# Reordering the start of a GRU and mixture-of-experts kernel: first loads, biases and the second block's projections

## The chip, the cores and the metric

The kernel runs on one core of one Trainium2 chip. The metric is device time in microseconds (us) of one execution; the median of three runs is 1541.6 us (1538.61 to 1542.06).

## What is computed

The input is x with 8 sequences of 256 steps and 512 features. A GRU runs over the steps of every sequence, its outputs go through a mixture of 8 experts (two chosen per token) plus a shared feed-forward part, and x is added to that. What matters here is the GRU cell:

```python
def cell(h, x):
    gi = x @ W_ih + b_ih
    gh = h @ W_hh + b_hh
    i_r, i_z, i_n = jnp.split(gi, 3, axis=-1)
    h_r, h_z, h_n = jnp.split(gh, 3, axis=-1)
    r = jax.nn.sigmoid(i_r + h_r)
    z = jax.nn.sigmoid(i_z + h_z)
    n = jnp.tanh(i_n + r * h_n)
    h_new = (1.0 - z) * n + z * h
```

`gi` doesn't depend on h, so it can be made ahead of the steps. The two biases of r and z can be added together into `gi`; of n, only b_ih goes into `gi`, and the last third of b_hh has to stay with `h_n`.

## The kernel before, in words

The 256 steps are cut into 16 blocks of 16 steps. For a block, x is a tile of 128 tokens by 512 features (`load_x`, L106). `transpose_x` (L256) turns it with four TensorE transposes into PSUM, ScalarE copies that to `xT` (L261), and the load of the block two further on is issued. `project(k, g)` (L294) makes the third g of the block's `gi`: four pieces, one for each 128 features of x, each of four matmuls of 32 columns of weights by 512 (`multiply`, L267; a float32 matmul shows as two records in the trace), and after the last piece VectorE adds the bias (L310) and, for the second and third g, SP issues a DMA of `gi` to DRAM (`gid_rz`, L319, `gid_n`, L321). `load_seeds` (L332) fetches it back in the layout of the steps, four steps at a time, `open_gate` (L349) has ScalarE copy one step's part into the three PSUM banks of the gates, and `step` (L360) multiplies the state by w_hh on top of it (three times 16 matmuls, L368), after which VectorE and ScalarE work out the new state.

The order of all of this is written by hand: every engine takes its instructions in the order in which the program issues them, and waits in place for what the next one needs. Ahead of the loop the program issues, in order, the loads and constants (L111 to L230), the transposes and projections of block 0 (L788 to L791), the transposition of the first state (L792), the seeds of the first eight steps (L794), the opening of the gates of step 0 (L798, in the order r, n, z) and the loads of the shared weights (L799). Then come the blocks. Everything that TensorE does beside the steps is cut into pieces that wait in `queue`; after each step, pieces are taken from it so that the block's share is spread evenly over its 16 steps (L851). Block 0 takes the projections of the next blocks, up to a quota of 2.8 times the cost of one (L831); later blocks take an even part of what is left, and the shared feed-forward part of the block before. Costs are counted in us: `MM` is 0.86 for a piece, `TR` 0.12 for a transpose.

The loads at the start: SP issues the three thirds of w_ih (L118, 1024 KB each), the four parts of w_hh (L132, 768 KB each) and the x of block 1 (L133). ScalarE issues the x of block 0 (L111). GpSimd (POOL) issues b_ih, broadcast from DRAM to all 128 partitions (L123), the first two thirds of b_hh in the same way (L125), the four parts of the first state h (L130), and later the last third of b_hh (L216). VectorE adds the two broadcast biases (L211).

Of the kernel before, what the change touches and what calls it, by code (L numbers as in the profile page):

```python
# [9 lines left out]
F32 = mybir.dt.float32  # L10
# [3 lines left out]
ALU = mybir.AluOpType  # L14
# [3 lines left out]
P = 128  # L18
# [7 lines left out]
def kernel(  # L26
# [46 lines left out]
    nc = tc.nc  # L73
    B, T, D = x.shape
# [4 lines left out]
    NQ = D // P  # L79
    NB = T // TS  # L80
# [17 lines left out]
    ps_mm = ctx.enter_context(tc.tile_pool(name="ps_mm", bufs=3, space=PSUM))  # L98
# [7 lines left out]
    def load_x(k, queue=nc.sync):  # L106
        xt = xpool.tile([P, D], F32, tag="x", name=f"x_{k}")
        queue.dma_start(xt, x[:, k * TS : (k + 1) * TS, :])
        x_tiles[k] = xt

    load_x(0, nc.scalar)  # L111


    we = wts.tile([P, E, NW, D], F32, name="we")
    wih = we[:, E - 2 : E].rearrange("p e w n -> p (e w n)").rearrange("p (q n) -> p q n", q=NQ)
    whh = we[:, E - 4 : E - 2].rearrange("p e w n -> p (e w n)").rearrange("p (q n) -> p q n", q=NQ)
    for g in range(3):
        nc.sync.dma_start(  # L118
            wih[:, :, g * D : (g + 1) * D],
            w_ih[:, g * D : (g + 1) * D].rearrange("(q p) n -> p q n", p=P),  # L120
        )
    bias = const.tile([P, G3], F32, name="bias")
    nc.gpsimd.dma_start(bias, b_ih.partition_broadcast(P))  # L123
    bias_h = we[:, 0, 0:2].rearrange("p w n -> p (w n)")
    nc.gpsimd.dma_start(bias_h, b_hh[0 : 2 * D].partition_broadcast(P))  # L125
    h = state.tile([P, NQ, 32], F32, name="h")
    nc.vector.memset(h, 0.0)
    h0v = h0.rearrange("b (q j i) -> b j q i", q=NQ, j=4)
    for j in range(4):
        nc.gpsimd.dma_start(h[32 * j : 32 * j + B], h0v[:, j])  # L130
    for q in range(NQ):
        nc.sync.dma_start(whh[:, q, :], w_hh[q * P : (q + 1) * P, :])  # L132
    load_x(1)  # L133
    wg = wts.tile([P, NQ, E], F32, name="wg")
    wsu = [wts.tile([P, NQ, 2, IM], F32, name=f"wsu_{c}") for c in range(NSH)]
    wsd = [wts.tile([P, NF, D], F32, name=f"wsd_{c}") for c in range(NSH)]
# [39 lines left out]
    def counting(name, n, base, step, channel):  # L176
# [31 lines left out]
        ]  # L208
        for i in range(NB)
    ]  # L210
    nc.vector.tensor_tensor(  # L211
        bias[:, 0 : 2 * D], bias[:, 0 : 2 * D], bias_h, ALU.add
    )
    b_hn = b_hh[2 * D : G3].rearrange("(q j i) -> j q i", q=NQ, j=4)
    for j in range(4):
        nc.gpsimd.dma_start(  # L216
# [39 lines left out]
    def transpose_x(k):  # L256
        ps = for_transposes([NQ, P], f"xTp_{k}")
        for q in range(NQ):
            nc.tensor.transpose(ps[:, q, :], x_tiles[k][:, q * P : (q + 1) * P], ident)  # L259
        xT = two.tile([P, NQ, P], F32, tag="xrT", name=f"xT_{k}")  # L260
        nc.scalar.copy(xT, ps)  # L261
        xT_of[k] = xT
        x_tiles.pop(k)
        if k + 2 < NB:
            load_x(k + 2)

    def multiply(ps, lhs, rhs, start, stop):  # L267


        for c in range(4) if by_groups[0] else (slice(0, P),):  # L270
            rows_ = slice(32 * c, 32 * c + 32) if by_groups[0] else c
            nc.tensor.matmul(  # L272
                ps[rows_], lhs[:, rows_], rhs, start=start, stop=stop, skip_group_check=True
            )
# [4 lines left out]
    def matmul_piece(issue, end=None):  # L279

        def part(cols, last):
            issue(cols)
            if last and end is not None:
                end()

        return (
            MM,
            lambda: part(slice(0, D), True),  # L290
            [(MM / 2, lambda i=i: part(HALVES[i], i == 1)) for i in range(2)],
        )

    def project(k, g):  # L294

        box = {}

        def issue(q, cols):
            if q == 0 and cols.start == 0:
                box["ps"] = ps_mm.tile([P, D], F32, tag="mm", name=f"gip_{k}_{g}")  # L300
            multiply(
                box["ps"][:, cols],
                xT_of[k][:, q, :],
                wih[:, q, g * D + cols.start : g * D + cols.stop],
                start=(q == 0 and cols.start == 0),
                stop=(q == NQ - 1 and cols.stop == D),
            )

        def end():
            nc.vector.tensor_tensor(  # L310
                gi[:, :, g, :].rearrange("p j (q i) -> p j q i", i=32),
                box["ps"].rearrange("p (q j i) -> p j q i", j=4, i=32),
                bias[:, g * D : (g + 1) * D].rearrange("p (q j i) -> p j q i", j=4, i=32),
                ALU.add,
            )
            if g > 0:
                to = gi_dram[k][g % 2].rearrange("j b t n -> (b t) j n")
                if g == 1:
                    nc.sync.dma_start(to.rearrange("p j (a n) -> p j a n", a=2), gi[:, :, 0:2, :])  # L319
                else:  # L320
                    nc.sync.dma_start(to, gi[:, :, 2, :])  # L321
                    projected.add(k)

        return [
            matmul_piece(lambda cols, q=q: issue(q, cols), end if q == NQ - 1 else None)
            for q in range(NQ)
        ]
# [131 lines left out]
    def weigh_all(k):  # L459

        ch, w2 = chosen.pop(k), weight_of.pop(k)
        comb = said_0[:, :, 1]
        nc.vector.tensor_scalar(comb, ch[:, 0, :], w2[:, 0:1], None, ALU.mult)
        nc.vector.scalar_tensor_tensor(comb, ch[:, 1, :], w2[:, 1:2], comb, ALU.mult, ALU.add)
        nc.vector.tensor_scalar(
            said_0[:, :, 0], row_of.broadcast_to([P, E]), 0.0, None, ALU.add
        )
# [29 lines left out]
    def enter(k, i):  # L497

        pl = places_of[k]
        nc.gpsimd.indirect_dma_start(  # L500
            out=listed.rearrange("r p v -> (r p) v"),
            out_offset=bass.IndirectOffsetOnAxis(ap=pl[:, i : i + 1], axis=0),
            in_=(said[k % 2] if k else said_0)[:, i, :],
            in_offset=None,
        )
# [281 lines left out]

    transpose_x(0)  # L788
    for g in range(3):
        for piece in project(0, g):  # L790
            piece[1]()  # L791
    nc.vector.transpose(states[0].rearrange("p q b -> p (q b)"), h.rearrange("p q i -> p (q i)"))  # L792
    for c in range(NS):
        load_seeds(c)  # L794
# [6 lines left out]
    projections = deque()  # L801
    projections.append((NQ * TR, lambda: transpose_x(1)))
    for k in range(1, NB):
        for g in range(3):
            projections.extend(project(k, g))
            if g == 1 and k + 1 < NB:
                projections.append((NQ * TR, lambda k=k: transpose_x(k + 1)))
    PROJECT = 12 * MM + NQ * TR
    for k in range(NB):


        at = {}

        def when(t, cost, work):
            at.setdefault(t, []).append((cost, work))

        if k > 0:
            steps_ = ((choose, 0.95), (order_experts, 0), (weigh, 0), (give_places, 0.1), (send_rows, 0.5))
            for t, (f, cost) in enumerate(steps_):
                when(t, cost, lambda f=f, k=k: f(k - 1))  # L820
            if k == 1:
                when(3, 0, lambda k=k: weigh_all(k - 1))
            for i in range(2 if k > 1 else E):
                when(i + 4, 0, lambda k=k, i=i: enter(k - 1, i))
            when(6, 0, lambda k=k: load_again(k - 1))
        if 1 <= k <= E - 4:
            when(6, 0, lambda k=k: load_expert(k - 1))
        if k == NB - 1:
            for e in (E - 2, E - 1):
                when(6, 0, lambda e=e: load_expert(e))  # L830
        quota = 2.8 * PROJECT if k == 0 else sum(p[0] for p in projections) / max(1, NB - 1 - k)  # L831
        while projections and quota > 0:
            quota -= projections[0][0]
            queue.append(projections.popleft())
        assert k == NB - 1 or len(projections) <= 13 * (NB - 2 - k), "the next block's are made"
        if k > 0:
            for c in range(NSH):
                feed_at_once(shared_unit(k - 1, c, NSH))
        over = 0.0
        for t in range(TS):  # L840
            n = k * TS + t
            step(n)
            if (n + 1) % SC == 0 and n + 1 < T:
                turn_seeds((n + 1) // SC)
                if (n + 1) // SC + NS - 1 < T // SC:
                    load_seeds((n + 1) // SC + NS - 1)
            for _, work in at.get(t, ()):
                work()

            later_on = sum(cost for s, pieces in at.items() if s >= t for cost, _ in pieces)  # L850
            room = (sum(p[0] for p in queue) + later_on) / (TS - t) - over  # L851
            room -= sum(cost for cost, _ in at.get(t, ()))
            while queue and room > 0.25 * MM:
                if len(queue[0]) > 2 and room < 0.75 * MM:
                    queue.extendleft(reversed(queue.popleft()[2]))
                piece = queue.popleft()
                piece[1]()
                room -= piece[0]
            over = -room if t < TS - 1 else 0.0
        fill()  # L860
# [3 lines left out]
    k = NB - 1  # L864
# [14 lines left out]
    while queue or routing:  # L879
        while routing and (spent >= routing[0][0] or not queue):  # L880
            routing.pop(0)[1](k)
        piece = queue.popleft()
# [36 lines left out]
```

## Time and profile before

| | us |
|---|---|
| median of three runs | 1541.6 (1538.61 to 1542.06) |
| the profiled execution | 1535.54 |
| its span | 1533.8 |
| TensorE busy | 1472.5 (96% of the span) |
| VectorE, ScalarE, GpSimd busy | 731.0, 435.5, 210.2 |
| start of the first projection's matmuls | 14.22 |
| start of step 0's matmuls | 35.61 |

The profile is one execution. The chain that ended last is followed back from the last instruction to whatever released each one, and "issue" in it is time in which an engine waited for nothing that the profile shows. "SPq", "ACTq" and "POOL ... DMA" are instructions that issue DMAs. A row of the timeline has start, length, engine, line, operation, output<-inputs and a count, and in brackets the idle time before it with what ended it. A row of a table of stretches has the length of the stretch, then the busy time and number of instructions of PE, PEld, DVE, ACT and POOL, then the granted TensorE clock as a share of full speed, the share of the DMA engines that was busy, and GB/s. A row of waits has who waited for whom, us in total, how many times, and the longest.

### The profile page before, as it was taken

Reading aid. Unit: us, or ns where it says so; the run is one execution under the profiler, and the core shown is the slowest. Engines: PE = TensorE matmul, PEld = TensorE weight load, DVE = VectorE, ACT = ScalarE, POOL = GpSimd, SP = SyncE. Lnnn points to the kernel's source line nnn. Section 1 sums busy time; section 2 is a strip of 40 time slices with the busy share of each in tenths; the row PEclk is TensorE's granted clock in tenths of the full one; section 3 lists DMA queues with packets and bytes.
Section 4 is the critical chain, followed back from the end, with each engine's and each line's share of the span. In section 5 each row is a group of like instructions: output and inputs, shape, how many; then the busy total and the mean of one; then the engine's idle time right before and its main releaser. Section 6 shows DMA issues by size and latency. Waiting matters only on the chain.

```text
span 1533.8 us, 82162 instructions
## 1 busy us (share of the span) xinstructions
PE 1472.5 (96%) x36779; PEld 1155.0 (75%) x36779; DVE 731.0 (48%) x2747; ACT 435.5 (28%) x1799; POOL 210.2 (14%) x419
## 2 busy tenths in 40 slices
PE   4999799999999999999999999999999999999997
PEld 1677678887879897879787989798889886444443
DVE  2455354545555545555555555555555553222222
ACT  1233232323232323333333333333333331222221
POOL 2001100000000000000000000100010102444443
PEclk9999999999999999999999999999999999999998
DMA  7613112121211111111111110101010214454544
GB/s 255 207 41 110 13 40 64 46 72 42 75 40 36 35 42 34 42 29 41 26 50 28 43 37 26 48 22 49 21 48 22 76 59 141 83 89 90 93 86 62
DMA packets 59168, 94.51 MB, mean 62 GB/s; under 512 B 8960, under 2 KB 29504, under 8 KB 58816
## 3 DMA queue, kind: packets, MB, share of 16 engines
q1 hardware_dynamic: 48056, 66.89, 15.1%
q0 software_dynamic: 10624, 22.10, 7.9%
q8 instruction: 290, 4.75, 1.3%
q14 instruction: 62, 0.51, 0.1%
q10 hardware_dynamic: 136, 0.26, 0.1%
HBM read 57.85 MB, written 31.37 MB: 58 GB/s over the span
## 4 chain that ended last, share of the span: by engine, by line
PE 95%; issue 2%; DMA 1%; ACT 0%; SPq 0%; DVE 0%; POOLq 0%; POOL 0%; DVEq 0%; ACTq 0%
PE ps_r L368 15%; PE gu_s L659 15%; PE ps_n L368 15%; PE ps_z L368 15%; PE gip L272 11%; PE gu_t L595 9%; PE po L272 7%; PE yp L731 4%; PE lgp L419 1%; DMA x<-in_x_dram 1%; PE xTp L259 1%; PE hrp L512 1%; PE ps_r L712 0%; PE ps_z L712 0%; PE ps_n L712 0%
## 5 line engine op out<-in xcount | busy, mean ns | idle before, releaser
L368 PE MATMUL ps_r<-we,hT 128*8 128x128 f32 x8192 | 294.8, 273 | 17.6 <-ACT ps_r L355 9.5
L368 PE MATMUL ps_z<-we,hT 128*8 128x128 f32 x8192 | 299.2, 273 | 5.6 <-issue 4.9
L368 PE MATMUL ps_n<-we,hT 128*8 128x128 f32 x8192 | 297.1, 273 | 2.9 <-issue 2.3
L368 PEld LDWEIGHTS ps_r<-we,hT 128*8 128x8 f32 x8192 | 240.4, 90 | 76.9 <-issue 32.8
L659 PE MATMUL gu_s<-hc,wsu 128*32 128x128 f32 x8192 | 281.0, 274 | 8.3 <-issue 7.9
L659 PEld LDWEIGHTS gu_s<-hc,wsu 128*32 128x32 f32 x8192 | 253.0, 110 | 30.1 <-issue 20.9
L368 PEld LDWEIGHTS ps_z<-we,hT 128*8 128x8 f32 x8192 | 242.2, 90 | 13.2 <-issue 11.5
L368 PEld LDWEIGHTS ps_n<-we,hT 128*8 128x8 f32 x8192 | 241.7, 90 | 8.7 <-issue 7.5
L387 ACT ACTIVATE r<-rT 128x32 f32<-128x32 f32 x256 | 58.6, 229 | 571.5 <-DVE rT L379 565.9
L407 POOL COPY hc<-hT 128x32 f32<-128x32 f32 x256 | 62.0, 242 | 1113.1 <-DVE hT L404 1113.1
L379 DVE STREAM_TRANSPOSE rT<-ps_r 128x128 f32<-128x128 f32 x256 | 80.8, 316 | 272.0 <-PE ps_r L368 271.1
L272 PE MATMUL gip<-we,xT 128*32 128x512 f32 (+1 forms) x1904 | 190.3, 516 | 1.4 <-ACT xT L261 1.4
L379 DVE STREAM_TRANSPOSE nT<-ps_n 128x128 f32<-128x128 f32 x256 | 81.1, 317 | 144.4 <-PE ps_n L368 144.2
L595 PE MATMUL gu_t<-we,xrT 128*128 x312 | 146.7, 593 | 0.2 <-ACT xrT L714 0.2
L272 PE MATMUL po<-wsd,act_s 128*32 128x512 f32 (+2 forms) x1108 | 138.8, 537 | 1.4 <-issue 1.4
L272 PEld LDWEIGHTS gip<-we,xT 128*32 128x32 f32 x1904 | 59.8, 110 | 66.3 <-issue 54.4
L355 ACT COPY ps_n<-seed_hn 128x128 f32<-128x128 f32 x256 | 69.0, 269 | 104.1 <-DVE nT L379 103.0
L379 DVE STREAM_TRANSPOSE zT<-ps_z 128x128 f32<-128x128 f32 x256 | 81.0, 316 | 18.1 <-PE ps_z L368 9.8
L588 DVE TENSOR_TENSOR act_t<-gu_t,act_t 128x256 f32<-128x256 f32 x39 | 16.5, 424 | 146.3 <-ACT act_t L587 146.3
L595 PEld LDWEIGHTS gu_t<-we,xrT 128*128 128x128 f32 x312 | 53.3, 190 | 38.7 <-issue 38.0
L395 ACT ACTIVATE nn<-nt 128x32 f32<-128x32 f32 x256 | 58.8, 230 | 82.5 <-DVE nt L393 81.2
L737 POOL DMA_INDIRECT out_dram<-y,row x39 | 61.6, 1579 | 125.3 <-DVE y L734 70.1
(157 smaller groups left out, 1186.8 us busy)
## 6 DMA issues: line engine op xcount, KB each, us to landing
gid_rz<-gi SPq DMA_DIRECT2D x16, 512.0 KB
seeds<-gid_rz SPq DMA_DIRECT2D x256, 32.0 KB
we<-in_L_ffn_w_gate_up_dram SPq DMA_DIRECT2D x8, 1024.0 KB
gid_n<-gi SPq DMA_DIRECT2D x16, 256.0 KB
seeds_n<-gid_n SPq DMA_DIRECT2D x256, 16.0 KB
wsu<-_L_ffn_w_sh_gate_up_dram SPq DMA_DIRECT2D x8, 512.0 KB
rows<-hr SPq DMA_DIRECT2D x16, 256.0 KB
again<-in_x_dram SPq DMA_DIRECT2D x16, 256.0 KB
```

The source lines that it names most:

```text
L272: nc.tensor.matmul(ps[rows_], lhs[:, rows_], rhs, start=start, stop=stop, skip_group_check=True)
L355: nc.scalar.copy(banks[g][:, 0:P], src[g])
L368: nc.tensor.matmul(bank[32 * j : 32 * j + B, 0:P].rearrange("p (a i) -> p a i", i=32), hT[:, q, 0:B], whh_v[:, q, lo : lo + NQ, j, :], sta ...
L379: nc.vector.transpose(gT.rearrange("p a b -> p (a b)"), banks[g][:, 0:P])
L387: nc.scalar.activation(r, gr, AF.Sigmoid)
L395: nc.scalar.activation(nn, nt, AF.Tanh)
L407: nc.gpsimd.tensor_copy(hc_of[k].rearrange("p q (b t) -> p q b t", t=TS)[:, :, :, t], new)
L588: nc.vector.tensor_tensor(act, ps[:, 0:IM], act, ALU.mult)
L595: nc.tensor.matmul(box["ps"], lhs(q), w_up(q), start=(q == 0), stop=(q == NQ - 1))
L659: nc.tensor.matmul(box["ps"][32 * g : 32 * g + 32, m, :], wsu[c][:, q, two_i, fs], hc_of[k][:, q, :], start=(m == 0 and q == 0), stop=(q = ...
L731: nc.tensor.matmul(box["y"], lhs, rhs, start=(f == 0), stop=(f == NF - 1))
L737: nc.gpsimd.indirect_dma_start(out=out.rearrange("b t d -> (b t) d"), out_offset=bass.IndirectOffsetOnAxis(ap=laid["row"][:, i : i + 1], a ...
```

## The change

Four things are changed. The x of block 0 is issued from SP ahead of w_ih, not from ScalarE; the x of block 1 is issued from SP after w_ih and ahead of w_hh. The biases are loaded as single rows into one partition (space of an expert's weights that is loaded later), by ScalarE's queue, and so is h; for each third of block 0's projection, a matmul of a row of ones with the bias row spreads the bias over 128 partitions in PSUM, the second bias is summed there by another such matmul, and ScalarE copies the sum to `bias`. This stands ahead of the last of the third's four pieces. The addition on VectorE goes. Last, the first nine pieces of the queue (the transposes of block 1's x, and the first two thirds of its projection, with what their ends issue) are issued ahead of the loop, after the gates of step 0 are opened and the shared weights are asked for; block 0's quota goes from 2.8 to 2.6.

```diff
-    load_x(0, nc.scalar)
+    load_x(0)
...
     bias = const.tile([P, G3], F32, name="bias")
-    nc.gpsimd.dma_start(bias, b_ih.partition_broadcast(P))
-    bias_h = we[:, 0, 0:2].rearrange("p w n -> p (w n)")
-    nc.gpsimd.dma_start(bias_h, b_hh[0 : 2 * D].partition_broadcast(P))
+    bias_row = we[0:1, 0, 0:3].rearrange("p w n -> p (w n)")
+    nc.scalar.dma_start(bias_row, b_ih.unsqueeze(0))
+    bias_h = we[0:1, 0, 3:5].rearrange("p w n -> p (w n)")
+    nc.scalar.dma_start(bias_h, b_hh[0 : 2 * D].unsqueeze(0))
...
     for j in range(4):
-        nc.gpsimd.dma_start(h[32 * j : 32 * j + B], h0v[:, j])
+        nc.scalar.dma_start(h[32 * j : 32 * j + B], h0v[:, j])
+    load_x(1)
     for q in range(NQ):
         nc.sync.dma_start(whh[:, q, :], w_hh[q * P : (q + 1) * P, :])
-    load_x(1)
...
-    nc.vector.tensor_tensor(
-        bias[:, 0 : 2 * D], bias[:, 0 : 2 * D], bias_h, ALU.add
-    )
+    one = we[0:1, 2, 0, 0:P]
+    nc.vector.memset(one, 1.0)
+
+    def spread_bias(g):
+        ps = ps_mm.tile([P, D], F32, tag="mm", name=f"biasp_{g}")
+        cols = slice(g * D, (g + 1) * D)
+        nc.tensor.matmul(ps, one, bias_row[:, cols], start=True, stop=(g == 2))
+        if g < 2:
+            nc.tensor.matmul(ps, one, bias_h[:, cols], start=False, stop=True)
+        nc.scalar.copy(bias[:, cols], ps)
...
     for g in range(3):
-        for piece in project(0, g):
+        pieces = project(0, g)
+        for piece in pieces[:-1]:
             piece[1]()
+        spread_bias(g)
+        pieces[-1][1]()
...
     PROJECT = 12 * MM + NQ * TR
+
+    for _ in range(1 + 2 * NQ):
+        projections.popleft()[1]()
...
-        quota = 2.8 * PROJECT if k == 0 else sum(p[0] for p in projections) / max(1, NB - 1 - k)
+        quota = 2.6 * PROJECT if k == 0 else sum(p[0] for p in projections) / max(1, NB - 1 - k)
```

## The prediction

> **What bounds the kernel now.** I read the page's busy shares first (TensorE 96%), then the chain that ended last: from 35.6 us on it is almost only matmuls, so the loop over the 256 steps is bound by the amount of work on TensorE, and what happens before step 0 is added to the end one for one. Here is that start in the chain of waits (start us, length us, what):
>
> ```profile
> 0.74 11.58 DMA x<-in_x_dram
> 12.46 1.10 PE xTp L259 x4
> 13.58 0.59 ACT xT L261
> 14.22 11.95 PE gip L272 x96
> 26.33 0.47 issue
> 26.92 3.39 DMA gid_n<-gi
> ...
> 32.73 2.45 DMA seeds<-gid_rz
> 35.28 0.28 ACT ps_r L355
> 35.61 1.89 PE ps_r L368 x32
> ```
>
> The first x lands only at 12.3 us. The twelve pieces of the first projection (96 records, two per matmul) end at 26.2. Then TensorE stands for 9.4 us: gi goes out to DRAM, comes back as seeds, and ACT copies it into the three banks. Two stretches of that, with the granted clock as the third figure from the right:
>
> ```profile
> 26.33:35.61 9.28, 0.00 (x1) 0.01 (x1) 1.49 (x3) 0.33 (x2) 0.00 (x0) 0.74 0.34 102
> 35.61:40.98 5.37, 5.37 (x97) 3.71 (x98) 1.01 (x4) 2.51 (x7) 0.00 (x0) 0.50 0.62 190
> ```
>
> TensorE does nothing in the first, and all of step 0 then runs at half clock: 5.37 us where a warm step takes 3 x 0.87 = 2.61. Next, ScalarE in order of time, because everything that TensorE waits for there passes through it:
>
> ```profile
> 0.74 1.21 ACTq L108 DMA_DIRECT2D x<-in_x_dram  x1
> 1.98 1.28 ACT L261 ACT_TABLE_LOAD   x1 [1.98 <-issue]
> 13.58 0.58 ACT L261 COPY xT<-xTp 128x512 f32<-128x512 f32 x1 [10.32 <-PE xTp L259]
> 35.28 0.27 ACT L355 COPY ps_r<-seeds 128x128 f32<-128x128 f32 x1 [21.12 <-DMA seeds<-gid_rz]
> 35.49 0.26 ACT L355 COPY ps_n<-seed_hn 128x128 f32<-128x128 f32 x1
> 35.69 0.26 ACT L355 COPY ps_z<-seeds 128x128 f32<-128x128 f32 x1
> 35.97 1.28 ACT L387 ACT_TABLE_LOAD   x1
> ```
>
> The order is that of the program: the copy into ps_n needs only seed_hn, yet it stands behind the one into ps_r, which waited 21 us for the seeds. Last, the waits of the DMA-issuing engines:
>
> ```profile
> SPq L108 <- DMA x<-in_x_dram: 2.3, 1, 2.3
> SPq L319 <- DMA we<-in_L_cond_W_ih_dram: 1.3, 1, 1.3
> ...
> POOL seed_hn L216 <- DMA bias<-in_L_cond_b_ih_dram: 2.8, 1, 2.8
> POOL seed_hn L216 <- DMA we<-in_L_cond_b_hh_dram: 2.0, 1, 2.0
> ```
>
> x_1 shares no buffer with x_0, but its load waited for x_0 to land. Counted in the program, x_0 (ACT), three of w_ih and four of w_hh (SP) are eight DMAs, and x_1 is the ninth; on POOL the ninth and tenth wait in the same way for the first and second. So I read that a DMA from SP or ACT, counted together, waits for the one eight before it, and its engine stands.
>
> **What the Trainium skill says.** "DMA: Bandwidth & Descriptors", section "Issuing engines are not separate DMA queues": SP, ACT and POOL share the same 16 engines and interleave. The trace agrees: x, 256 KB, took 11.58 us on ACT's queue beside w_ih and the broadcasts. "TensorE: Matmul & The Clock Gate", Part 1: half clock by default, full clock after a busy window of about 3.4 us that runs freely. The trace agrees: after 14.22 the weight loads of the first projection are 0.85 us per group of four for some 3 us, then 0.43; step 0 was cold for all its 5.37. "ScalarE: Activation LUTs", section "ACT is a hardware spline evaluator": the compiler places a table load right before the activation that needs it; here both stand directly before theirs, at 1.28 us each. As a price, "TensorE: Matmul & The Clock Gate", section "Why this matters for your kernels": a matmul with K of 32 takes as long as one with 128. No run here shows a K of 1.
>
> **Part 1: x ahead of w_ih.** x and the first third of w_ih are 256 + 1024 KB = 1.31 MB. SP's queue moved 0.05 MB by 2.5 us and 0.86 MB from 2.5 to 5; at the 0.20 MB per half us of its steady slices the other 0.40 are through at 6.0. From the last bytes to landing x took about 0.5 us, the second third of w_ih up to 1.6 (its bytes were through at about 13.5, SP was let go at 15.09); I take 0.9, so 6.9. x lands at about 4 and its transposes (1.10) are done by 5.3. That is 7 us better than now.
>
> **Part 2: biases by rows.** The broadcasts (768 + 512 KB on POOL) are gone, and so is the 1.22 us addition on DVE; it is off the path. POOL is free 3.6 us earlier, which hides too: ident is needed only when x lands. Added are six DMAs on ACT in place of x's one, ahead of the table load and the copy of xT. By the count of eight, the last of h is the tenth and waits for w_ih's first third, 6.9 us. Then its issue 0.5 (small ones on SP take 0.33, those of h on POOL 0.55), the table load 1.28, the copy 0.58 and a handover of 0.06: TensorE starts the projection at 9.3, not 6.9 (bounds 6.6 if ACT isn't held, 10.5 if w_ih lands late). w_hh waits for w_ih's last third by the same count; its 3 MB at 0.4 MB/us still land by about 22, before gi is complete, so I cost that at nothing; if they came after 27 they would delay gi's DMA.
>
> The five matmuls of ones: the nearest row is yp, 128x128 weights by 512 columns, four records (two matmuls) in 1.72 us:
>
> ```profile
> 1309.46 1.88 PE L731 MATMUL yp<-we,actT_t 128*128 x4
> 1311.18 0.60 PE L712 MATMUL ps_r<-ident,xr 128*128 128x128 f32 x4
> ```
>
> That is 0.86 each, 4.3 us for five, all on the path, since TensorE has its weights from then on. Below 0.86 I see no way (the price above); above, cold ones cost double, which the cold term holds. The ACT copies (0.58) hide behind the last piece (0.86).
>
> Sum: 9.3 + 12 pieces x 0.86 = 10.3 + 4.3 + cold loss. Cold now cost 11.95 - 10.3 = 1.6; by the free window 1.6 to 3.2; I take 2.4. The first projection ends at 26.3, against 26.2 now. **The early x is used up** by ACT's wait, the matmuls of ones and a colder start.
>
> **Part 3: nine pieces ahead of step 0.** In the program they follow the three openings of the gates. The transposes of x_1 run at once, but their ACT copy stands behind ps_r, which waits for the seeds; so the eight projection pieces can't fill the gap, and step 0 stands behind them on TensorE. From the end of the projection to the opening is 35.28 - 26.2 = 9.1: opening at 35.4. Then three copies 0.67, xT 0.58, handover 0.05: TensorE begins at 36.7, where step 0 began at 35.6. Eight pieces 6.9, step 0 warm 2.6, cold loss 2.4 (1.6 to 3.2): 48.6. Before, the same work was complete at 42.29 (step 0 cold, transposes, a 0.75 us wait for xT) + 6.9 = 49.2. Gain 0.6.
>
> What else moves: the load of x_3 and the second gid_rz now stand on SP behind the shared weights, which SP finishes issuing at about 51; the next seeds are asked for only after step 3 (59.7 now), so it hides. The table load for the sigmoid hides behind the eight pieces. Block 0 has 2.6 x 10.8 = 28 us of filler over 16 steps, 1.75 a step; from the end of z to the next state takes about 1.25 (46.4 to 47.65), so no step is laid bare. The 1.55 us gap of TensorE at 53.95, with nothing waited for, fell while the shared weights landed; now slow-issuing pieces stand there. I count half of it: 0.6.
>
> Gain 1.2 in all. The profiled execution took 1535.54 (span 1533.8), 6.1 below the median of 1541.6; taken off that, 1540.4.
>
> **The rivals.** B, ACT isn't held (the count of eight is not as I read it): start at 6.9, 2.4 sooner, so 1538.0. For: only one DMA stood on ACT before. Against: SP's and POOL's waits. C, the gap is filled as arranged: step 0 at 35.7, warm or half cold, done by 39.5 where 49.2 was: 9.7 gained, with the half gap 1531.3. It needs ACT to copy xT ahead of the gates; the order in the trace speaks against it. D, **slower**: TensorE's gaps called "issue" grow. They total some 24 us over the loop, the longest 3.3, with 12.6 us idle in 130 to 240, where the chain shows no engine to wait for. New instructions and moved pieces shift where they fall. Three more of 1.65 give 5 us: 1545.4; it decides from 4.3 us of new gaps. Against: the stream changes by a few dozen records in 73,000.
>
> **Numbers.** My case 0.60, B 0.16, C 0.07, D 0.17. This kernel's measurement can tell 0.2%, 3.1 us, from no change. My case (own range 1537.5 to 1543.5) gives faster 0.10, same 0.48, slower 0.02; B 0.11 faster, 0.05 same; C all faster; D 0.14 slower, 0.03 same: 0.28, 0.56, 0.16. The range 1536.2 to 1545.0 leaves out C and the far half of D.
>
> **What would show it.** The first gip record at about 9.3 (6.9: B); the last DMA of h issued just after w_ih lands; five pairs of biasp records at 0.86 each; the first projection ending near 26.3; xT of x_1 copied directly after ps_z and not before; step 0 after 16 x 4 records of gip, at full clock. I am wrong if xT_1 is copied before the seeds land, if w_hh holds gi's DMA, or if "issue" gaps change by over 3 us.

## The result, and the profile after

The changed kernel takes 1551.3 us where the kernel before takes 1540.6 (medians of 12 runs each, 1541.6 to 1557.3 and 1535.2 to 1546.6): the ratio is 1.007, interval 1.005 to 1.009. It is slower by some 11 us. 1540.4 was predicted, and 1545.0 was the end of the range.

The profiled execution of the kernel after took 1553.9 (span 1552.1), 2.6 above its median; that of before, 1535.5, was 5 below its own. The two traces are therefore 18.3 us apart in span, more than the kernels are, and every size below that comes from the two traces alone is too large in the same way.

First the start, in the chain of waits of the kernel after (start us, length us, what):

```profile
1.60 6.81 DMA we<-in_L_cond_W_ih_dram
8.55 4.88 PE gip L282 x24
13.43 1.05 PE biasp L219 x2
14.48 0.86 PE biasp L221 x2
...
27.29 2.29 DMA gid_n<-gi
...
32.00 2.42 DMA seeds<-gid_rz
35.22 0.52 ACT xT L271
35.79 9.20 PE gip L282 x64
44.99 0.88 PE ps_r L378 x32
```

TensorE starts at 8.55 instead of 14.22, held now by w_ih's first third. The matmuls of ones (`biasp`) and a slow first third of the projection (4.88 us for three pieces) use up what was won, so the last piece ends at 26.48 (26.2 before). Then the copy of xT stands where the program put it, behind the three gates, in ScalarE's timeline of the kernel after (start, length, operation, in brackets the idle time before it):

```profile
1.56 2.95 ACTq L132 DMA_DIRECT2D h<-in_cond_dram  x4
4.54 1.28 ACT L271 ACT_TABLE_LOAD   x1 [4.54 <-DVE first_place L183]
7.27 0.59 ACT L271 COPY xT<-xTp 128x512 f32<-128x512 f32 x1 [1.44 <-PE xTp L269]
...
34.56 0.27 ACT L365 COPY ps_r<-seeds 128x128 f32<-128x128 f32 x1 [8.50 <-DMA seeds<-gid_rz]
...
34.96 0.26 ACT L365 COPY ps_z<-seeds 128x128 f32<-128x128 f32 x1
35.16 0.58 ACT L271 COPY xT<-xTp 128x512 f32<-128x512 f32 x1
```

So the gap stays empty, and the eight pieces run from 35.79 to 44.82. Step 0 is warm after that (2.73 us) and ends at 47.6; before, the same work would have been done at 49.2, by the prediction's sum. The start is 1.6 us better, and the loss must come later.

Block 1 begins at 119.0 (114.6 before). Counting the projections' pieces in both traces, the kernel after has 51 of them behind it there and the one before 45; six pieces by 0.86 are 5.2 us, so it is still ahead by 0.8. Blocks 1 to 14 then take 1092.2 us where they took 1077.8, with those six pieces less to do. **In the loop 14.4 + 5.2 = 19.6 us are lost between these two traces.** TensorE's waits in that part show where; first before, then after (who waited for what: us in total, times, longest):

```profile
PE gu_s L659 <- issue: 7.9, 7, 3.3
PE ps_r L368 <- issue: 7.3, 6, 1.9
PE ps_z L368 <- issue: 2.8, 7, 1.3
PE ps_n L368 <- issue: 2.3, 4, 1.0
```

```profile
PE gu_s L669 <- issue: 8.8, 9, 2.6
PE ps_r L378 <- issue: 8.2, 8, 2.3
PE ps_n L378 <- issue: 7.8, 13, 2.3
PE ps_z L378 <- issue: 7.0, 9, 3.1
```

In all four rows TensorE waits for nothing that another engine does. Counted one by one in blocks 1 to 15, gaps of this kind over 0.3 us were 14 with 19.3 us, and there are now 32 gaps with 33.9: 14.6 more. With some of the longest the clock falls to half for 3.40 us, here in the table of stretches of the kernel after (the third figure from the right):

```profile
159.60:163.00 3.40, 3.40 (x72) 3.16 (x68) 0.85 (x2) 0.38 (x1) 0.41 (x1) 0.50 0.60 16
326.80:330.20 3.40, 2.96 (x49) 2.39 (x51) 0.66 (x4) 0.58 (x3) 0.00 (x0) 0.51 0.08 23
```

In the same 15 blocks the kernel before had one such stretch and the kernel after has four; three more, at half of 3.4 each, are 5 us. Block 15 became longer as well (71.8 us before, 73.3 after), so these 14.6 + 5 stand against a loss of 21.

**What the gaps wait for.** One of them, in TensorE's timeline of the kernel after, and then the transfers of 184.5 to 187 us in that trace:

```profile
187.84 1.58 PE L669 MATMUL gu_s<-hc,wsu 128*32 128x128 f32 x49 [1.95 <-issue]
```

```profile
DMA packets 1, 0.02 MB, mean 7 GB/s; under 512 B 0, under 2 KB 0, under 8 KB 0
...
q8 instruction: 1, 0.02, 3.7%
```

A single packet of 16 KB moved, on the queue named "instruction". That it is TensorE's own next instructions follows from the count below. It started at 184.81 and took 1.47; TensorE ran out at 185.89 and went on at 187.84, 1.56 after the packet's end. The page of the kernel after has 289 packets on that queue and TensorE 74,110 records, one packet to 256 records. I numbered TensorE's records (matmuls, weight loads and the 644 of its sequencer together) and set each gap beside the packet ahead of its end. These are the gaps of the kernel after of 1.7 us and more:

```text
gap from  length  next record  mod 256  packet from  took  gap ends after its end
  155.89    2.60         6081      193       156.10  0.93     1.46
  168.29    2.33         6593      193       168.25  1.00     1.36
  180.48    1.73         7106      194       179.79  0.95     1.48
  185.89    1.95         7361      193       184.81  1.47     1.56
  192.06    1.70         7617      193       191.34  0.88     1.54
  245.59    1.79        10433      193       245.09  0.92     1.37
  324.14    3.10        15041      193       324.71  1.08     1.45
  407.35    2.10        19649      193       407.19  0.88     1.38
 1241.17    3.06        68801      193      1241.86  1.00     1.38
```

Of the 32 gaps 28 (32.1 of the 33.9 us) lie at this one place of every 256 records, and all 14 of before do. So "issue" is here the wait for the next page of instructions (a page is 256 records, and the place in it is the record's number modulo 256). The gaps lie in the steps with the shared unit's matmuls (gu_s), where a page is used up in about 3.5 us; the closest two packets start 3.2 us apart. In these steps there is little to spare, and a packet that starts late leaves TensorE standing: ahead of the 28 gaps the packet started 2.6 us (median) after the last page's end had been passed, ahead of all other page ends 0.6.

Waits shorter than 0.3 us count too. I added up the time from each record to the next by its place in the page, for blocks 1 to 14. Before, the eight places from 192 on took 22.9 us more than eight of the other places do in the mean; after, 38.7 more. **Of the 14.3 us by which these blocks grew, 15.8 are waits at the page's end and 3.4 the half clock; the rest of the time fell by 4.9, which is the work of the six pieces.** With that the 19.6 are accounted for.

### The profile page after: what moved, and what is told of

The parts are those of the page before. It is cut to its first block, busy times and chain, and to the rows that moved or that the text cites. A ratio compares the mean times of both kernels' runs of the same rounds, so it can differ in the third digit from the quotient of the medians.

```text
span 1552.1 us, 82076 instructions
## 1 busy us (share of the span) xinstructions
PE 1484.6 (96%) x36733; PEld 1158.2 (75%) x36733; DVE 731.8 (47%) x2747; ACT 437.1 (28%) x1802; POOL 207.6 (13%) x413
## 4 chain that ended last, share of the span: by engine, by line
PE 94%; issue 3%; DMA 1%; another core or an unknown queue 0%; ACT 0%; SPq 0%; DVE 0%; POOLq 0%; POOL 0%; ACTq 0%; DVEq 0%
PE ps_n L378 15%; PE ps_r L378 15%; PE ps_z L378 15%; PE gu_s L669 15%; PE gip L282 11%; PE gu_t L605 9%; PE po L282 7%; PE yp L741 4%; PE lgp L429 1%; PE hrp L522 1%; PE xTp L269 1%; DMA we<-in_L_cond_W_ih_dram 0%; PE ps_r L722 0%; PE ps_z L722 0%
## 5 line engine op out<-in xcount | busy, mean ns | idle before, releaser
L378 PE MATMUL ps_n<-we,hT 128*8 128x128 f32 x8192 | 301.7, 273 | 8.4 <-issue 7.8
L378 PEld LDWEIGHTS ps_z<-we,hT 128*8 128x8 f32 x8192 | 243.2, 90 | 13.9 <-issue 12.1
L605 PEld LDWEIGHTS gu_t<-we,xrT 128*128 128x128 f32 x312 | 53.3, 190 | 38.7 <-issue 38.0
```

The lines of the kernel that those rows point to most:

```text
L378: nc.tensor.matmul(bank[32 * j : 32 * j + B, 0:P].rearrange("p (a i) -> p a i", i=32), hT[:, q, 0:B], whh_v[:, q, lo : lo + NQ, j, :], sta ...
L605: nc.tensor.matmul(box["ps"], lhs(q), w_up(q), start=(q == 0), stop=(q == NQ - 1))
```

## The experiments

The rivals were, in the order in which they came up: one part of the change alone is to blame; block 0's new quota leaves fewer pieces to the later blocks; the small scattered DMAs (`enter`, which write a block's picked tokens to DRAM beside the steps) delay the refills; **the place** decides, that is, which instructions of a step a page's end falls on. Times are medians; ratios are to the kernel before on the same chip, with their 95% interval. They are not the quotients of two medians and differ from these by up to 0.3%.

**The parts.** The first and second part without the third:

```diff
-    for _ in range(1 + 2 * NQ):
-        projections.popleft()[1]()
...
-        quota = 2.6 * PROJECT if k == 0 else ...
+        quota = 2.8 * PROJECT if k == 0 else ...
```

> Parts 1 and 2 alone: x ahead of w_ih and the biases by rows, no pieces ahead of step 0, the quota of block 0 back at 2.8. Theory 1 (less projection work left for blocks 1 to 14, so that their steps of fast small matmuls outrun the refill of TensorE's instructions): the later blocks are as before, and the start is 0.7 us shorter (gates opened at 34.6 in the changed kernel, 35.3 before): 0 to 2 us faster than before. Theory 2 (the instruction stream of TensorE is longer by ten matmuls' records and POOL issues six DMAs less, which shifts where refills fall): 5 to 12 us slower.

1547.7, ratio 1.0027 (1.0010 to 1.0045). The third part alone, on the kernel before:

```diff
+    for _ in range(1 + 2 * NQ):
+        projections.popleft()[1]()
...
-        quota = 2.8 * PROJECT if k == 0 else ...
+        quota = 2.6 * PROJECT if k == 0 else ...
```

> Part 3 alone: the nine pieces ahead of step 0 and the quota of 2.6, with the first loads and biases as before. Theory 1: the start gains 0.8 us, the later blocks have 5.2 us less projection work and lose 10 to 14 us in gaps: 8 to 13 us slower than before. Theory 2: no matmul is added, so about as before, within 2 us.

1559.5, ratio 1.0101 (1.0070 to 1.0133). Each part alone is slower, and the two don't add up: their sum is 1.3%, the whole 0.7%. No part is the culprit by itself.

**The quota.** Counting the pieces made ahead of the loop, in block 0, and in blocks 1 to 14: before 12, 33, 147; after 20, 31, 141. Two kernels put the sharing of the one into the other:

```diff
-        quota = 2.6 * PROJECT if k == 0 else ...
+        quota = 2.8 * PROJECT - (8 * MM + NQ * TR) if k == 0 else ...
```

> The changed kernel, but with block 0's quota cut by the cost of the nine pieces, so that blocks 1 to 15 have exactly the projection pieces that they had before (block 0 has 22.4 us of them in place of 28). Theory 1: the gaps of the later blocks are as before, and the kernel is 1 to 2 us faster than before. Theory 2: as slow as the changed kernel, 8 to 12 us over before.

The change with the old sharing (147 pieces in blocks 1 to 14): 1543.9, ratio 1.0020 (1.0006 to 1.0035). Most of the loss goes.

```diff
-        quota = 2.8 * PROJECT if k == 0 else ...
+        quota = 2.6 * PROJECT + (8 * MM + NQ * TR) if k == 0 else ...
```

> The kernel before, with block 0's quota raised to what the changed kernel has made by the end of block 0 (35.9 us by its own costs in place of 30.2), so that blocks 1 to 15 have the pieces of the changed kernel. Nothing else is changed. Theory 1: 8 to 14 us slower than before, with gaps in steps 6 and later of the blocks. Theory 2: within 2 us of before.

The kernel before with the new sharing (141): 1549.3, ratio 1.0069 (1.0042 to 1.0096): the whole loss, with nothing else of the change. That made fewer pieces the favourite. If it were that, more pieces in the later blocks should be no loss:

```diff
-        quota = 2.8 * PROJECT if k == 0 else ...
+        quota = 2.8 * PROJECT - 6 * MM if k == 0 else ...
```

> The kernel before, with block 0's quota cut by six pieces (27 in place of 33), so that blocks 1 to 14 have six pieces more (153) where the changed kernel has six less (141). If projection pieces in the later blocks are what gives the refill time: 4 to 10 us faster than before, the mirror of e4_quota_up. If only a cut costs (the blocks of before have all they need): within 3 us of before.

152 pieces, five more: 1555.4, ratio 1.0116 (1.0081 to 1.0152), worse than either. **Fewer pieces as the only cause falls**; what all changes of the quota have in common is that from block 1 on the instructions stand elsewhere in their pages.

**The scattered DMAs.** Both kernels without `enter`. They leave out the listing of almost all tokens for the experts, whose part of the output is then missing; TensorE's matmuls are the same in number:

```diff
-            for i in range(2 if k > 1 else E):
-                when(i + 4, 0, lambda k=k, i=i: enter(k - 1, i))
```

> The changed kernel without the small scattered DMAs (enter, L507) that POOL issues inside the blocks: 8 in block 1, 2 in each later one. This leaves out the listing of the tokens of all blocks but the last for the experts, so that the tile part works on rows of weight 0; the matmuls are the same in number. Theory A (while such a DMA is under way, the refill of TensorE's instructions starts late, and steps of fast small matmuls run dry): gaps in blocks 1 to 14 fall from 32 us to under 8, and the kernel is 20 to 30 us faster than the changed one, about 1520 to 1530. Theory B (the refill is at its limit in these steps by itself, whatever POOL does): gaps and time as in the changed kernel, within 5 us.

> The kernel before without the same DMAs (the same part is left out). Theory A: gaps in blocks 1 to 14 fall from 18 us to under 5, 12 to 18 us faster than before, and the distance to the changed kernel without them turns round: the changed one is then 0 to 2 us faster, by its start. Theory B: within 5 us of before, and the changed one still some 10 us slower.

After 1528.8, ratio 0.9912 (0.9882 to 0.9943); before 1518.4, ratio 0.9852 (0.9822 to 0.9883). They cost both kernels 22 to 23 us, so they do matter; in block 1 the idle time of TensorE (gaps over 0.15 us) falls from 13.5 to 3.3 us in the one and from 10.5 to 2.4 in the other. In the kernel after, 16 of the 28 gaps at a page's end had such a DMA issued shortly before (from 3 us ahead of the last page's end to the start of the late packet); of the other page ends 6% had. But the two kernels are 10 us apart without `enter` as with it. The DMAs are not the difference. Nor is that pair's difference all in the waits: of the 9.4 us that the changed kernel loses there in blocks 1 to 14 (4.2 us longer, with 5.2 of work less), 4.0 are waits at the page's end and 3.4 half clock; 2.0 stay open.

**The place.** The kernel before with small matmuls added ahead of step 0, whose results nobody reads. First in float32, four records each, five of them (here) and then 32:

```diff
+    for _ in range(5):
+        nc.tensor.matmul(
+            banks["r"][:, 0:32], seeds[0][:, 0, 0:P], seeds[0][:, 0, 0:32], start=True, stop=True
+        )
```

> The kernel before, with five small matmuls added beside the three that open the banks (20 more instructions for TensorE, as many as the matmuls of ones are, run in its first 8 idle us), nothing else. If the place of the refills in the stream is what made e1_xbias some 4 us slower: 3 to 8 us slower than before, or as much faster. If it isn't (the stretch of the stream is neutral, and it is what POOL, SP or ACT issue differently): within 2 us of before.

> The same with 32 small matmuls (128 more instructions, half of what one refill brings). They keep TensorE busy in part of the time in which it waits for x, which may warm its clock for up to 1.6 us of gain at the start. If the place of the refills matters: a time that differs from e9_shift20 by 3 us or more after that is taken off. If not: 0 to 2 us faster than before.

The 20 records: 1545.5, ratio 1.0020 (1.0004 to 1.0035). The 128: 1553.1, ratio 1.0088 (1.0064 to 1.0113), but they ran until 17.3 and put off step 0 by 5 us, so 6 to 9 us remain for the place (by the medians or by the ratio). The cleaner pair has tiny bfloat16 matmuls of two records each, over by 7.1 us, long ahead of the first projection: 64 for half a page (here), then 128 for a whole one:

```diff
+    tiny = seeds[0][:, 0, 0:P].bitcast(BF16)
+    for _ in range(64):
+        nc.tensor.matmul(banks["r"][0:8, 0:8], tiny[:, 0:8], tiny[:, 0:8], start=True, stop=True)
```

> The kernel before with 64 tiny bf16 matmuls (128 instructions, half a refill), which unlike those of e10_shift128 end before x lands. Theory 2: 6 to 9 us slower than before, and e15_before_plus256 isn't. If both are as before, the cost of e10_shift128 was its start alone.

> The kernel before with 128 tiny bf16 matmuls (256 instructions, one whole refill) in TensorE's idle start. Theory 2: all refills fall where they fell, the time is that of before within 2 us (they may warm the clock for up to 1.6 us). Theory 3: 3 us or more slower, like the other shifts.

Half a page: 1551.7, ratio 1.0066 (1.0043 to 1.0089), with step 0 at 35.4 as before. A whole page: 1541.3, ratio 0.9990 (0.9975 to 1.0005). Twice as many instructions cost nothing: every later one stands at its old place in a page. Rows of TensorE's waits from 36 to 1220 us, with half a page and then with a whole one:

```profile
PE gu_s L662 <- issue: 19.2, 12, 4.0
```

```profile
PE gu_s L662 <- issue: 10.4, 7, 2.8
PE ps_r L371 <- issue: 8.9, 6, 3.3
```

All rows of "issue" together are 31.3 us with half a page, 26.8 with a whole one and 21.3 before. These are single executions (1557.8, 1544.7 and 1535.5, where the medians are 1551.7, 1541.3 and 1542.2), and the waits differ from one execution of a kernel to the next, so the medians carry the comparison. The clock adds to it: from 50 to 1300 us, half a page has 20.5 us at half clock, a whole page 3.4, as before. What the traces do show is the place: nine of the 14 gaps of before, with 16.0 of their 19.3 us, stand in the run with a whole page at the same instruction, 256 records on.

**This is the one clean proof in the set: in the kernel before, the place of the page ends alone is worth 10 us**, as much as the change lost. The same half page (the 64 tiny matmuls) in the changed kernel:

> The changed kernel with 64 tiny bf16 matmuls (128 instructions, half a refill) in TensorE's idle start; they may delay the transposes of x by up to 2 us. Theory 2 (the place of the refills): the loss is drawn anew, the time differs from the changed kernel's (some 11 us over before) by 3 us or more, more likely down, since few places are worse: 1540 to 1548. Theory 1 (six pieces fewer in the later blocks): as the changed kernel, 1550 to 1554.

1545.8 beside 1535.1 on that chip, ratio 1.0053 (1.0027 to 1.0079). By the ratio that is 1.7 thousandths better than the change by itself, by the medians the same 10.7 us behind the kernel before, and the intervals overlap. A change of 3 us or more was expected from the place; it decides nothing.

**The same pieces in another order.** The projection's pieces go in after the shared unit's first part of the block, not ahead of all four; quota and number of pieces are those of the change:

```diff
         if k > 0:
+            mine = list(queue)
+            queue.clear()
             for c in range(NSH):
                 feed_at_once(shared_unit(k - 1, c, NSH))
+                if c == 0:
+                    queue.extend(mine)
```

> The changed kernel, with the order of a block's pieces changed: the first shared unit, then the block's projection pieces (long matmuls, few instructions), then the other three shared units. So the scattered DMAs at steps 4 and 5, and the steps after them, meet long matmuls; in block 1, with eight such DMAs at steps 4 to 11, only the first half does. Theory A: the gaps at steps 6 and 7 of blocks 2 to 14 go (18 us in the changed kernel, to under 6), 8 to 14 us faster than the changed kernel. Theory B: gaps move to the first steps of the blocks, where the small matmuls now stand, with the same sum.

1542.6, ratio 1.0006 (0.9994 to 1.0019). Block 1 starts at 118.6 as in the change (119.0), and blocks 1 to 14 take 1082.2 us instead of 1092.2. The loss is gone, within the interval, without a piece being added or removed. That speaks against the number of pieces as the only cause; the order and the places changed together, so it doesn't tell these two apart.

**The gap.** The transposes of x_1, and with them ScalarE's copy, ahead of the gates, with the old sharing of the pieces:

```diff
+    transpose_x(1)
     for g in banks:
         open_gate(0, g)
...
-    projections.append((NQ * TR, lambda: transpose_x(1)))
...
-    for _ in range(1 + 2 * NQ):
+    for _ in range(2 * NQ):
...
-        quota = 2.6 * PROJECT if k == 0 else ...
+        quota = 2.8 * PROJECT - (8 * MM + NQ * TR) if k == 0 else ...
```

> The changed kernel with the quota of e3_quota_back, and with the transposes of the second block's x and their ACT copy issued ahead of the opening of step 0's gates, so that the eight projection pieces can run while the seeds are fetched. The start theory of the prediction (only ACT's order keeps the gap empty): the projection pieces run from about 27.5 to 35, step 0 starts at about 35 at full clock, 10 us ahead of the changed kernel, and with the later blocks as in e3_quota_back the time is 9 to 11 us under that kernel, about 1533. Rival: something else (a buffer of PSUM, gi) holds the pieces, and the time is that of e3_quota_back within 2 us.

1535.9, ratio 0.9971 (0.9955 to 0.9988). The eight pieces run from 28.1 to 35.2, and step 0 begins at 35.2, warm. Two variants of it follow, and one of the change with the old sharing. The first has the pieces spread over the first 13 of the shared unit's 24 in place of being put ahead of them:

```diff
+            theirs, both, n = list(queue), [], len(mine)
+            queue.clear()
+            for i, piece in enumerate(theirs):
+                while mine and (n - len(mine)) * 13 <= i * n:
+                    both.append(mine.pop(0))
+                both.append(piece)
+            queue.extend(both + mine)
```

> The kernel of e8_xT_ahead (gap filled, later blocks with their pieces of before), and in each block the projection pieces spread between the first 13 of the 24 shared pieces, not ahead of them all. If the rate at which a stretch asks for instructions sets the gaps: gaps at steps 6 and 7 mostly gone, 8 to 16 us under e8_xT_ahead's 1536, 1520 to 1528. If the gaps come from what is issued at steps 4 to 6 whatever runs: within 4 us of e8_xT_ahead.

1538.8, ratio 0.9999 (0.9983 to 1.0014): no gain over the kernel before that is clear of the interval, and 0.3% behind the last where 8 to 16 us of gain were expected. And 24 more records (12 of the tiny matmuls), after which block 1 begins at the same record of a page as in the kernel before (159 of 256; it was 135), in the kernel with xT ahead and in the change with the old sharing:

> The kernel of e8_xT_ahead, whose blocks 1 to 15 have the queue of before but start 24 instructions earlier within a refill, with 12 tiny bf16 matmuls (24 instructions) in TensorE's idle start. Theory 2 (the place of the refills): the later blocks cost what they cost before, so the 11 us gained at the start show: about 1530, 5 to 7 us under e8_xT_ahead. Theory 3 (any disturbance is as good as another, and 24 of 256 is too little to matter): as e8_xT_ahead, 1536, within 2 us.

> The same for e3_quota_back, which starts its later blocks 25 instructions earlier within a refill than before. Theory 2: 3 to 5 us under e3_quota_back, 1539 to 1541, at or just under the kernel before. Theory 3: as e3_quota_back, 1544, within 2 us.

1537.6, ratio 0.9967 (0.9955 to 0.9980), and 1543.2, ratio 1.0008 (0.9992 to 1.0024). Neither differs from its original by more than the intervals, where 3 to 7 us of gain were expected from the place. The first of them began block 1 at 110.0, 4.6 us ahead of the kernel before, and by the medians (1537.6 beside 1542.2) all of that was left at the end. Its blocks 1 to 15 stand at the places of before, and 13 of the 14 gaps of before are in its trace at the same instruction. Last, the two edits that worked, together: xT ahead of the gates and the order by parts, with the change's quota of 2.6.

> The stream of e7_after_slow_at_enter on TensorE, unchanged, with ACT's copy of the second block's x ahead of the gates as in e8_xT_ahead, and block 0's quota left at 2.6 so that its steps stay covered. By the start alone 10 to 11 us under e7_after_slow_at_enter (which was 0 to 2 us over before): about 1532, 9 us under the kernel before. If something else than the refill places made the other kernels lose their start, it is 1536 or more.

**1521.2 beside 1535.1, ratio 0.9907 (0.9887 to 0.9927): 14 us better than the kernel before**, where 9 were expected, and the best of all the runs that leave nothing out. ScalarE's timeline, then the chain, both of this kernel:

```profile
26.44 0.58 ACT L271 COPY xT<-xTp 128x512 f32<-128x512 f32 x1 [1.00 <-PE xTp L269]
33.94 0.27 ACT L365 COPY ps_r<-seeds 128x128 f32<-128x128 f32 x1 [6.91 <-DMA seeds<-gid_rz]
```

```profile
31.38 2.41 DMA seeds<-gid_rz
34.26 1.06 PE ps_r L378 x32
```

The copy now comes 7.5 us ahead of the first gate, not behind the last, and step 0 begins at 34.26 with 20 pieces done, where before it began at 35.61 with 12. Block 1 starts at 110.2; with the six pieces more that are done by then, that is 4.4 + 5.2 = 9.6 us ahead of the kernel before. Blocks 1 to 14 take 1068.7, 9.1 less than before with 5.2 of work less, so 3.9 more are won. The sum is 13.5 of the 13.9 measured. One thing in it is not explained: the run with the order by parts but without the early copy has TensorE's records of every block at the same places of a page to within two, and its blocks 1 to 14 took 1082.2, 13.5 us longer. The place is not all that decides.

## Why the prediction was wrong

- **What bounds it: right.** The loop is bound by TensorE, and the start counts one for one. But the loop's time is not only a sum of work: the waits between the matmuls, and the clock after them, depend on the program's layout.
- **Part 1: right in the order, off in size.** w_ih's first third landed at 8.4, not 6.9, and x at about 6, not 4, with its transposes done at 7.2, not 5.3. As the first third was later still, only that one counts.
- **Part 2: near in sum, wrong in how.** The sum had ScalarE held until w_ih's first third lands. It was not: its last DMA of h was issued by 4.51. That is what rival B forecast. That w_ih came 1.5 us late hid the error in the time: luck. The projection waited for w_ih itself, until 8.55 (9.3 predicted, 6.9 under rival B). The five matmuls of ones took 4.9 us (4.3 predicted): 1.91 for each pair with the second bias, 1.05 for the last. The earlier start and the longer run cancel: the end came at 26.48, 26.3 was predicted. The semaphores in the trace show what became of the count of eight: each DMA of SP and ScalarE reuses that of the one eight before it, as read, but in an order that runs over both engines and is not that of the program. The last of h is the ninth in it and follows b_ih's small row, which had landed; w_ih's last third is the tenth, and for it SP stood until x had landed (who waited for what: us in total, times, longest):

```profile
SPq L118 <- DMA x<-in_x_dram: 3.5, 1, 3.5
```

- **Part 3: right.** xT directly after ps_z, the pieces from 35.79 (36.7 predicted, gid_n landed in 2.29 and not 3.39), the same work complete at 47.6 (48.6 predicted, 49.2 before). Rival C was rightly ruled out for this order of the program, and its mechanism is real: with the copy ahead, the gap fills, and in the last experiment that is most of the gain.
- **"I count half of it: 0.6": wrong.** Half of 1.55 is 0.8, and the gap in block 0 didn't shrink; there was one of 2.27, with another of 0.54 ahead of it. Slow-issuing pieces beside it were no cure. Of the 1.6 us that the start won, 0.8 were left when block 1 began.
- **The step that failed is the end of the sum**, "Gain 1.2 in all": it costs the moved pieces and the 20 added records at nothing from block 1 on. The argument for it stood under rival D: "Against: the stream changes by a few dozen records in 73,000." It is not the number that counts, but the place: in the kernel before, shifting the 74,000 records by half a page cost 10 us where a whole page cost none. What the runs showed instead: in the traces, the waits at the page ends of blocks 1 to 14 grew by 15.8 us, and the loss by half clock by 3.4. Rival D named the right symptom, with three gaps more of 1.65 us; there were 18 more, and three more stretches at half clock, which it left out: by the medians about 12 us instead of 5 (the 10.7 between the kernels, and the 1.6 that the start won).

Settled is where the time went between the two traces: into waits for instruction pages, in the steps that issue fastest, and into the clock after them. That moving the places alone does as much is shown on the kernel before. **Open** is how the change's own loss divides between the places and the six pieces that its later blocks have less. Each edit of the quota moved both, fewer pieces and more pieces were both slower, and half a page on top of the change settled nothing. Why a packet starts late in one step and not in a like one isn't shown either; a DMA of `enter` close by goes with it in about half of the cases. Of the shifts tried apart from all else, half a page cost 10 us and 6 to 9 (beside its late start), 20 records 3; 24 records on two other kernels and half a page on the change were within the intervals; none was a gain. So the kernel before may stand at one of the better places; six tries don't prove it.

## What to carry to other kernels

When an engine waits for "issue", number its records and look for one residue mod 256, and look for the 16 KB packet that ended just before: if both are there, the engine waits for its own instructions, and an edit ahead of that point can move such gaps by more than a small edit is worth. Test a small edit then with a padding of half a page and of a whole one beside it, before its own worth is believed or denied. To fill a gap, look at the in-order queue of every engine that the filler passes through: here eight pieces of TensorE's work stayed out of an idle 9 us for the sake of one 0.58 us copy on ScalarE, and moving that copy did what moving the pieces did not.

## What the runs showed of the hardware

- TensorE's instructions come in 16 KB packets, one for every 256 records (289 packets, 74,110 records). A packet takes 1.0 us in the median, and a gap that waited for one ends 1.2 to 1.6 us after its end; behind no page's end in blocks 1 to 15 did a record come sooner than 1.1 us after its packet. "Runtime: NRT & Kernel Launch", section "Instruction fetch mechanics", of the Trainium skill describes these blocks and calls the cost of a boundary "mostly hidden". Here 14 boundaries in 290 (before) and 28 in 289 (after) were not hidden by over 0.3 us each, up to 4.0 us in the kernel with half a page more.
- Such a gap can also cost the clock: in the kernel after, 3.4 us at half speed go with the gaps of 3.10, 3.06, 2.60 and 1.70 us, but not with those of 2.33 and 2.10. "TensorE: Matmul & The Clock Gate", Part 1, has the clock fall after an idle window of about 3.4 us; here single gaps of less were enough, so the length of one gap doesn't decide alone.
- Small DMAs that TensorE's matmuls do not wait for slow it all the same: without the scattered writes of `enter`, 22 us less in both kernels.
